# A two-layer transformer block beside a gated recurrence: the last product made token-major, the first root moved off GpSimd

## The chip, the cores and the metric

The kernel runs on one core of one Trainium2 chip. The metric is the device time of one execution in microseconds (us); the time before is the median of three runs. Profile names: PE is TensorE's matmuls, PEld its weight loads, DVE is VectorE, ACT is ScalarE, POOL is GpSimd, SP is SyncE, whose queue issues the DMAs. PSUM is the memory that TensorE writes and that DVE and ACT can read.

## The reference

The input `x` is 16 sequences of 512 tokens with 128 channels, in float32. What is computed, cut to the main lines:

```python
xn = layernorm(x)
# branch 1: gated recurrence
xc = causal_depthwise_conv(xn)                    # four taps
r, i = sigmoid(xc @ W_r.T + b_r), sigmoid(xc @ W_i.T + b_i)
a = sigmoid(log_a) ** (8 * r)
h[t] = a[t] * h[t-1] + sqrt(1 - a*a)[t] * (i * xc)[t]
s = rmsnorm(h @ W_out.T) * gamma
# branch 2: two layers of windowed attention (8 heads of 64, window 64) and a gated feed-forward block
for l in range(2):
    y = shift_token(z)                            # z starts as xn; half the channels one token later
    q, k, v = split(y @ wqkv[l])                  # q, k: l2norm, scale, rotary
    z = z + attention(q, k, v) @ wo[l]
    y = layernorm(shift_token(z)) * ln_g + ln_b
    a, g = split(y @ w1[l] + b1[l])               # 341 columns each
    z = z + (a * gelu(g)) @ w2[l] + b2[l]
return x + s * silu(z)
```

## The kernel before

The program is a list of 6240 tasks, each of them a few instructions of one engine. A task is a name and an item: a sequence `s` (0 to 15), a tile `(l, n)` of 128 tokens in layer `l`, a pair of tiles `(l, m)`, or a chunk `(c, s)` of the feed-forward block. The table `PLACES` gives each task its place in the list (the numbers are steps from one item to the next), written out in numbers; `OPENED` gives the PSUM bank of each tile (7 banks that all tiles share). The list is issued in this order, so each engine's queue runs its tasks in order, and an engine whose next task is not ready waits although later ones are.

What the change and the prediction touch:

- **Start of a sequence.** `ld` loads `xtok`. `fbn` and `fag` are DVE's statistics (4 and 4 small instructions, `fmv`). `fpw` (`deviation`, L589 to L593) makes 1/sqrt(var + eps) and -mean/deviation on POOL, in four instructions on 128x4, one of them a power. `fnm` (`normalised`, L600) scales on ACT in four pieces of 128x128 tokens by channels. `ftx` transposes on PE to channel-major, `xp` (L648) copies on ACT, `xs0` and `xs1` (L644) make the residual stream `xS` on POOL. `dr0` (L515, L516) computes `e` from `log_a` on ACT, `dr` (L520 to L531) the decay rate from it on DVE; both happen once.
- **Attention** of each tile: `Q`, `K`, `V` on PE (helper `matmul`, L636), squares on ACT, rotary products on DVE (L728, L731) and sums on POOL (`addq`, `addk`, L735), the normalisation of q and k on POOL (`nrm`, L772), flips on PE (`tr`, L793), scores, DVE's maxima (L840), ACT's exponentials (L847), POOL's shares (L861), `PT`, `PV`, and at last `wo` and `y` (L907), which adds to `xS`.
- **Feed-forward** of each sequence: `tx`, statistics, `pw`, `nm`, `nr`, `th`, `hT`; then for three chunks of hidden columns `g` and `a` (PE), `ge` (gelu, ACT), `hi` and for the last chunk `hj` (DVE, L952 and L957, tile `hid`), and `yy`, the second product (`narrow`, tile `1y` in layer 1). It is channel-major: `w2` is the stationary operand, the 512 tokens of `hid` stream through.
- **End of a sequence in layer 1.** `r0` and `r1` (`residual`, L970) add bias and stream to `1y`, half the channels each, into `lx`. `tf` (L631) transposes `lx` on PE into two banks, tokens on partitions. `silu` (L978, L980): ACT's tanh (`tn`) and DVE's product (`z`), once a bank, into `th`. `zs` and `zx` (`combine`, L987) multiply by `s` and add `x` on POOL. `xld` reloads `x`, one buffer for all sequences; `ot` (L990) stores.
- **Elsewhere:** `wide` (two masks and `gamma`) is loaded and cast by `cm` on POOL; `yo` (in `recurrent`, L636) is the recurrence's output product, token-major, with stationary `h` and 128 streaming columns.

Of the kernel before, what the change touches and what calls it, by code (L numbers as in the profile page):

```python
# [9 lines left out]
F32 = mybir.dt.float32  # L10
BF16 = mybir.dt.bfloat16
I32 = mybir.dt.int32
AF = mybir.ActivationFunctionType
# [27 lines left out]
    "dr0": "11",  # L41
    "dr": "15",
    "l1": "8",
    "t0": "31",
    "cm": "36",
    "l2": "30",
    "t1": "91",
    "wb0": "90",
    "bb0": "101",
    "ws0": "97",  # L50
    "wb1": "95",
    "bb1": "108",
    "ws1": "109",
    "ld": "0 1 11 5 24 159 161 50 1015 184 315 507 472 367 183 574",
    "fbn": "2 3 18 70 128 66 97 42 1027 214 283 539 437 370 178 610",
    "fag": "4 3 18 81 136 57 105 39 1270 53 198 625 541 219 129 655",
    "fpw": "6 3 18 121 103 53 112 30 1332 -8 197 730 530 124 133 713",
    "fnm": "10 4 20 158 162 49 1019 176 318 505 475 340 209 570 341 226",
    "ftx": "13 5 26 282 40 1023 190 303 450 526 371 204 554 351 206 502",
    "xp": "16 5 26 291 35 1020 194 297 454 525 379 195 554 351 205 502",  # L60
    "xs0": "19 5 55 303 40 987 182 328 452 500 378 364 438 434 203 446",
    "xs1": "22 11 215 391 -212 978 319 453 352 393 457 348 344 402 374 236",
    "c0": "26 2 61 258 41 1010 209 283 453 548 356 194 562 346 204 513",
    "cv": "20 38 101",
    "c1": "35 30 114 183 36 1008 207 284 450 552 360 188 561 352 202 511",
    "c3": "40 28 116 188 49 994 217 273 454 552 363 179 568 360 197 509",
    "gr": "46 34 241 154 119 857 247 272 413 555 350 220 525 379 199 535",
    "sr": "52 51 240 177 87 861 239 273 436 533 348 218 532 370 200 535",
    "gi": "55 20 182 123 188 877 199 297 423 564 352 210 555 350 206 497",
    "si": "59 23 184 121 197 871 196 305 439 551 340 210 579 328 207 493",  # L70
    "ea": "56 63 264 299 323 470 343 212 751 182 343 602 319 208 494 378",
    "in": "63 39 208 85 201 864 194 311 459 526 339 212 578 329 210 495",
    "a2": "70 63 307 265 367 416 355 246 742 144 348 714 197 297 426 399",
    "m": "84 166 195 295 346 507 269 348 670 138 396 745 83 526 211 452",
    "rt": "275 18 201 462 552 186 412 264 719 8 680 436 345 231 473 466",
    "u": "295 17 198 476 532 184 458 221 720 5 697 418 360 226 463 465",
    "sc": "306 26 248 422 521 185 500 183 723 94 607 411 362 243 466 449",
    "yo": "311 46 280 388 506 197 517 153 723 149 595 413 321 240 475 495",
    "s2": "320 48 284 383 503 195 520 160 714 151 603 404 321 240 474 501",
    "ms": "324 50 284 382 506 190 522 159 717 153 597 407 321 239 477 503",  # L80
    "mp": "331 55 284 375 523 178 514 163 721 146 603 418 310 236 475 521",
    "ss": "337 55 312 349 523 178 516 161 722 151 596 437 290 236 473 523",
    "c2": "365 41 1004 215 273 456 553 357 185 568 352 198 511",
    "Q": "29 10 66 13 23 9 73 16 41 178 76 67 102 65 86 64 146 50 91 64 169 58 141 32 167 90 117 59 102 108 116 69 "
    "98 67 105 58 178 57 112 50 180 86 90 66 88 51 132 49 135 145 115 86 120 64 110 18 125 122 114 44 90 132 102 33 "
    "-5071 40 75 62 121 52 85 75 130 62 92 62 186 61 110 118 131 52 98 77 172 60 91 48 135 53 99 33 187 48 136 129 "
    "136 59 74 78 165 6 105 59 231 42 106 68 166 43 106 48 181 53 90 66 137 67 116 45 216 -4 48 3 88 7 49 33",
    "sqq": "42 7 72 14 26 15 80 16 24 184 60 76 111 57 98 59 134 57 94 56 166 69 130 43 167 85 111 71 127 78 113 73 "
    "91 72 111 51 171 62 115 58 188 65 96 70 88 51 131 43 137 143 126 71 135 50 110 24 124 119 123 38 97 119 101 48 "
    "-5081 47 72 78 101 59 95 57 141 64 76 72 176 71 106 119 131 46 109 60 184 59 87 64 119 58 96 26 196 56 126 141 "  # L90
    "131 62 70 66 183 20 83 55 226 52 117 74 151 27 128 50 172 47 86 66 150 51 133 66 185 8 47 4 87 -4 51 45",
    "rq1": "48 -3 71 10 45 36 42 5 62 153 97 44 105 58 100 61 145 45 94 58 168 61 147 21 173 92 118 53 113 101 113 "
    "71 94 72 103 57 183 51 118 45 186 75 101 65 111 22 152 31 135 141 113 104 118 50 112 37 111 114 118 54 112 98 "
    "108 26 -5070 62 62 73 104 69 66 99 107 67 93 58 181 63 123 107 133 62 91 76 165 62 99 45 127 58 97 52 168 48 133 "
    "138 138 52 80 104 131 28 90 71 211 48 116 79 149 39 103 60 175 105 26 86 124 67 118 58 193 2 62 -10 92 6 47 57",
    "rq2": "38 22 53 10 51 35 22 28 54 150 97 48 101 69 82 66 144 51 95 61 165 67 133 42 160 90 114 72 94 105 128 59 "
    "97 67 109 57 172 56 117 60 177 76 93 91 86 23 138 45 143 141 112 94 114 63 106 43 104 119 120 55 100 129 78 36 "
    "-5070 46 87 41 120 62 75 75 144 65 76 71 178 63 126 106 123 81 76 74 168 66 85 61 133 69 84 27 183 54 130 130 "
    "136 64 89 68 164 -6 107 61 226 53 96 76 161 52 108 34 180 119 25 89 127 62 109 68 194 3 54 -4 85 6 47 42",
    "addq": "54 12 62 10 70 17 49 102 26 94 91 55 86 67 97 111 100 35 111 118 110 80 101 71 120 94 125 83 145 32 160 "  # L100
    "57 107 41 101 99 157 35 125 120 147 34 105 82 119 19 113 67 193 48 167 90 94 50 104 38 193 20 138 89 61 165 55 "
    "43 -5099 66 74 81 102 39 102 88 106 108 28 113 173 18 195 62 115 115 71 104 95 121 59 39 138 86 63 46 157 86 167 "
    "114 96 79 90 96 149 -28 96 157 135 49 121 127 79 63 157 105 53 110 46 100 121 42 130 110 144 -8 75 27 32 10 47 "
    "91",
    "K": "37 27 46 15 48 -18 78 13 40 175 86 74 96 55 115 53 129 51 94 59 168 62 137 69 138 85 114 70 111 89 133 53 "
    "98 69 111 52 195 41 111 54 187 75 90 82 68 65 118 58 130 145 151 61 107 65 107 24 123 118 131 31 94 125 101 39 "
    "-5076 46 90 47 126 42 88 74 132 69 80 80 168 65 130 98 127 54 98 74 182 50 102 40 132 65 87 44 178 58 133 128 "
    "143 45 79 97 147 24 83 66 225 45 113 59 167 38 117 45 182 53 83 68 136 64 116 60 202 -4 54 24 70 28 17 35",
    "sqk": "43 26 55 8 46 -3 85 10 30 183 84 59 104 59 116 39 134 49 94 57 179 75 121 66 157 87 96 70 115 80 133 67 "
    "81 70 116 47 205 34 109 81 172 63 89 86 85 56 125 39 144 141 140 61 108 85 87 40 117 119 124 31 90 124 119 28 "  # L110
    "-5066 44 77 59 127 41 81 70 136 74 79 69 167 75 132 89 139 60 80 75 202 43 98 57 112 78 73 45 170 58 148 118 143 "
    "50 81 94 142 32 83 64 222 40 120 75 154 29 131 30 197 39 90 69 131 77 127 54 176 2 52 21 69 47 3 52",
    "rk1": "57 20 43 31 43 -7 78 14 15 179 91 72 87 59 119 59 123 48 94 62 160 66 132 96 112 93 117 80 91 96 140 46 "
    "91 75 103 59 194 48 104 62 176 97 80 77 70 61 123 50 128 142 164 59 123 49 109 17 132 103 141 33 103 107 109 42 "
    "-5080 41 92 48 121 60 66 89 118 73 76 96 157 60 146 97 117 62 108 72 174 47 98 49 134 64 74 46 178 63 133 119 "
    "144 100 26 98 143 31 79 78 228 34 109 59 182 63 75 50 187 68 76 54 130 74 126 58 199 -8 70 7 67 45 17 38",
    "rk2": "50 31 55 17 32 6 80 -10 31 185 78 78 91 53 116 60 121 63 90 54 169 70 128 83 120 102 99 81 106 88 146 38 "
    "100 68 105 63 188 53 99 90 155 86 84 70 72 66 129 44 156 121 153 64 132 36 106 22 139 107 126 29 103 123 101 31 "
    "-5073 55 90 40 127 67 68 85 113 85 69 87 156 65 133 98 121 60 103 95 157 51 98 61 111 70 81 62 166 59 123 131 "
    "151 67 70 99 135 12 82 70 220 57 109 70 153 55 107 42 177 72 77 59 144 62 119 57 192 15 69 21 37 30 26 38",  # L120
    "addk": "61 24 58 15 55 5 63 116 -6 93 127 49 88 73 115 58 93 71 96 96 114 118 81 99 94 103 116 118 78 81 140 62 "
# [179 lines left out]
}  # L301

OPENED = {
    "wb0": "5",
    "wb1": "2",
    "ftx": "01232346010245104151450443430562",
    "c0": "3601015300330",
    "cv": "452",
    "gr": "4315262451000334",
    "gi": "3621315416303611",  # L310
    "yo": "3555154434312536",
# [816 lines left out]
```

## Time and profile before

| | |
|---|---|
| median of 3 runs | 1288.69 us (1287.65 to 1289.12) |
| the profiled execution's own time | 1286.86 us |
| its span, first to last instruction | 1285.1 us |
| granted TensorE clock, mean | 0.996 |
| busy: PE, ACT, DVE, POOL | 1244.4, 1164.9, 1112.3, 1081.9 us |

"Busy" is the time in which an engine works on at least one instruction. The profile writes each matmul of the program on float32 as two records, and the two column halves of a product run beside each other, so a mean duration of a record is longer than the distance between the starts of two. "Idle before, releaser" tells what ended an engine's wait. In the timeline each row is start, duration, engine, line, operation and tiles, with what ended the wait in brackets; instructions of one line that follow each other are merged (x2).

### The profile page before, as it was taken

What the parts mean: (1) busy time and instruction counts of PE and PEld (TensorE: products, weight loads), DVE (VectorE), ACT (ScalarE), POOL (GpSimd) and SP (SyncE); (2) the same over time, 40 slices, a digit from 0 to 9 for tenths busy, and PEclk for the clock granted to TensorE, in tenths of its full rate; (3) what the DMA queues carried; (4) which work ended last, traced back from release to release, by engine and by line L of the source; (5) the groups of instructions that cost most, each with busy time, mean ns of one, the idle gap of its engine ahead of it and who ended that gap; (6) DMA issues with size and microseconds to landing.
All of it is one profiled execution on the core that took longest, in us unless ns stands there. A gap on an engine that the chain in (4) does not pass through costs nothing.

```text
span 1285.1 us, 45136 instructions
## 1 busy us (share of the span) xinstructions
PE 1244.4 (97%) x17672; PEld 697.2 (54%) x17672; DVE 1112.3 (87%) x2866; ACT 1164.9 (91%) x3776; POOL 1081.9 (84%) x1057
## 2 busy tenths in 40 slices
PE   7899999999999999999999999999999999999997
PEld 2455565645645555555555555655465555665463
DVE  7999989888898989898899989969998888858964
ACT  5989999998999999998989999998999899998793
POOL 7999998986889889898788998868998798975792
PEclk9999999999999999999999999999999999999998
DMA  6211021111202101102121011211111021120111
GB/s 191 47 35 27 6 48 22 27 31 46 47 15 72 35 22 40 32 10 55 39 51 31 18 31 28 52 31 39 30 25 41 18 47 30 32 64 10 35 44 37
DMA packets 46771, 49.50 MB, mean 39 GB/s; under 512 B 4704, under 2 KB 31456, under 8 KB 46560
## 3 DMA queue, kind: packets, MB, share of 16 engines
q1 hardware_dynamic: 46560, 46.63, 15.0%
q8 instruction: 140, 2.29, 0.7%
q14 instruction: 71, 0.58, 0.1%
HBM read 13.05 MB, written 4.19 MB: 13 GB/s over the span
## 4 chain that ended last, share of the span: by engine, by line
PE 49%; DVE 18%; ACT 15%; POOL 12%; issue 4%; DMA 0%; POOLq 0%; DVEq 0%; ACTq 0%
ACT pr L847 7%; PE q L636 5%; PE o L882 5%; PE x L900 5%; PE v L636 4%; PE sA L834 4%; PE k L636 4%; POOL rot L735 3%; PE p L869 3%; POOL rot L772 3%; PE t L793 3%; DVE norms L740 3%; DVE max L840 2%; PE 0g L636 2%; POOL pr L861 2%
## 5 line engine op out<-in xcount | busy, mean ns | idle before, releaser
L735 POOL TENSOR_TENSOR rot<-rot,sw 128x512 f32<-128x512 f32 x256 | 326.9, 1289 | 27.7 <-DVE rot L728 11.0
L861 POOL TENSOR_TENSOR pr<-pr,sum 128x512 f32<-128x512 f32 x256 | 266.2, 1050 | 72.9 <-DVE sum L855 42.9
L772 POOL TENSOR_TENSOR rot<-rot,y 128x1024 f32<-128x1024 f32 x128 | 243.3, 1905 | 21.8 <-DVE y L767 20.5
L847 ACT ACTIVATE pr<-sB,max 128x128 f32<-128x128 f32 x512 | 188.8, 437 | 6.3 <-DVE max L840 4.5
L847 ACT ACTIVATE pr<-sA,max 128x128 f32<-128x128 f32 x512 | 188.4, 434 | 3.5 <-DVE max L840 2.6
L740 DVE TENSOR_REDUCE norms<-sq 128x16 f32<-128x1024 f32 x128 | 156.0, 1219 | 5.9 <-ACT sq L721 3.7
L873 ACT COPY pT<-p 128x512 f32<-128x512 f32 x256 | 143.4, 653 | 13.4 <-PE p L869 12.8
L882 PEld LDWEIGHTS o<-pT,vl 128*64 128x64 f32 x2048 | 111.7, 137 | 50.2 <-issue 26.6
L847 ACT ACTIVATION_READ_ACCUMULATOR pr<-sB,max 128x1 f32 x512 | 136.5, 276 | 0.0
L636 PE MATMUL q<-wqkv,xS 128*64 128x512 f32 x512 | 134.2, 608 | 1.3 <-DVE cols L916 0.4
L834 PE MATMUL sA<-kT,qT 64*64 64x128 f32 x2048 | 135.1, 269 | 0.0
L847 ACT ACTIVATION_READ_ACCUMULATOR pr<-sA,max 128x1 f32 x512 | 134.3, 273 | 0.0
L834 PE MATMUL sB<-kT,qT 64*64 64x128 f32 x2048 | 133.5, 269 | 0.0
L636 PE MATMUL v<-wqkv,xS 128*64 128x512 f32 x512 | 132.1, 600 | 0.7 <-ACT pr L847 0.7
L636 PE MATMUL k<-wqkv,xS 128*64 128x512 f32 x512 | 131.6, 596 | 0.2 <-ACT pr L847 0.2
L882 PE MATMUL o<-pT,vl 128*64 128x64 f32 x2048 | 127.6, 223 | 0.6 <-ACT pT L873 0.2
L882 PE MATMUL o<-pT,vs 128*64 128x64 f32 x2048 | 126.3, 222 | 0.0
L834 PEld LDWEIGHTS sA<-kT,qT 64*64 64x64 f32 x2048 | 121.0, 133 | 8.2
L900 PE MATMUL x<-oT,wo 128*64 128x257 f32 x1024 | 123.0, 382 | 0.5 <-ACT oT L890 0.3
L834 PEld LDWEIGHTS sB<-kT,qT 64*64 64x64 f32 x2048 | 120.1, 133 | 0.0
L840 DVE TENSOR_REDUCE max<-sA 128x4 f32<-128x512 f32 x128 | 86.9, 681 | 23.3 <-PE sB L834 16.2
L882 PEld LDWEIGHTS o<-pT,vs 128*64 128x64 f32 x2048 | 104.6, 138 | 0.2 <-ACT pT L873 0.2
(169 smaller groups left out, 3207.4 us busy)
## 6 DMA issues: line engine op xcount, KB each, us to landing
vl<-vs SPq DMA_DIRECT2D x224, 128.0 KB, 2.3
xtok<-in_x SPq DMA_DIRECT2D x16, 256.0 KB, 3.0
x<-in_x SPq DMA_DIRECT2D x16, 256.0 KB, 3.4
out<-th SPq DMA_DIRECT2D x16, 256.0 KB, 2.9
wqkv<-in_wqkv SPq DMA_DIRECT2D x2, 768.0 KB, 6.8
w<-in_w SPq DMA_DIRECT2D x2, 384.0 KB, 6.4
rot<-in_rope SPq DMA_DIRECT2D x1, 512.0 KB, 5.7
wo<-in_wo SPq DMA_DIRECT2D x2, 256.0 KB, 5.2
```

What stands on the lines that cost most here:

```text
L636: nc.tensor.matmul(ps[col : col + 64], w[:, col : col + 64], v, start=start, stop=stop)
L735: nc.gpsimd.tensor_tensor(r, r, at["sw", *n, "qk"[i]], ALU.add)
L740: nc.vector.tensor_reduce(at["nx", *pair(n)][:, 0, 16 * j : 16 * j + 16], sq, AX.X, ALU.add)
L772: nc.gpsimd.tensor_tensor(flat, flat, bc(at["y", *pair(n)][:, 0, 16 * j : 16 * j + 16], DH), ALU.mult)
L793: nc.tensor.transpose(four(at["bank", f"t{w}", *n])[:, i, p, :], r[rows, i, 2 * p : 2 * p + 2, :], c["ident"][rows, rows])
L834: nc.tensor.matmul(out_(w, par)[:, p, :], q[r, p, half[w]], k[r, p, col : col + P], start=False, stop=p == 3)
L840: nc.vector.tensor_reduce(at["max", *n, h], sim, AX.X, ALU.max, negate=True)
L847: nc.scalar.activation(at["pr", *n][:, g, :], sim[:, p, :], AF.Exp, bias=at["max", *n, h][:, p : p + 1], accum_out=at["sum", *n][:, g : g ...
L861: nc.gpsimd.tensor_tensor(w, w, bc(at["sum", *n][:, g], P), ALU.mult)
L873: nc.scalar.copy(at["pT", *n][:, w], heads(ps))
L882: nc.tensor.matmul(o[64 * par : 64 * par + 64, p, 64 * w : 64 * w + 64], at[("vl", "vs")[w], *n][:, h * DH : (h + 1) * DH], pT[:, w, 4 * p ...
L900: nc.tensor.matmul(ps[64 * r : 64 * r + 64, 0 : 2 * P + 1], w, o[:, k, 1 - r : 2 * P + 2 - r], start=k == 0, stop=k == 3)
```

## The change

1. In layer 1, `narrow` makes the second product token-major: `hid` is now stationary in pieces of 64 tokens, and the 128 columns of `w2` stream. The sum in the bank `1y` has tokens on partitions.
2. The transposes `tf` no longer follow the residual: they turn the stream `xS` before the second product, and a new DVE task `xt` adds the bias (now along the free dimension, `b2_row`) and keeps the result in `lx`. `r0` adds `lx` to the product in its bank; `r1` of layer 1 is gone. `tn` and `z` then work on all 512 columns at once, from `1y`.
3. For sequence 0 alone, `fpw` becomes `fq` (a square root on ACT) and `fr` (a reciprocal and a product on DVE); of the four pieces of the normalisation two stay on ACT (`fnm`) and two go to DVE (`fnd`).
4. For the last sequence alone, `zs` and `zx` run on DVE.
5. `wide` has a fourth part of 128 columns, the bias of layer 1, which POOL copies to `b2_row`; a constant `eps` is set.
6. All of `PLACES` and `OPENED` is written anew, so the order of all tasks is another.

The diff's core (the tables and the entries of `do` are left out):

```diff
-        add(s, ("ld", [("xtok", s)]), ("fbn", [("fmv", s)]), "fag", "fpw", ("fnm", [("xnf", s)]))
+        add(s, ("ld", [("xtok", s)]), ("fbn", [("fmv", s)]), "fag")
+        add(s, *(["fq", ("fr", [("xnf", s)]), "fnd", "fnm"] if s == 0 else ["fpw", ("fnm", [("xnf", s)])]))
...
-                add(C, (p + "yy", [] if c else [("bank", p + "y", s)] + [("lx", s)] * l))
-            add(s, p + "r0", p + "r1")
+                add(C, (p + "yy", [] if c else [("bank", p + "y", s)]))
+            if l:
+                add(s, ("tf", two("tf", s)), ("xt", [("lx", s)]), p + "r0")
+            else:
+                add(s, p + "r0", p + "r1")
...
+    def first_deviation(s, part):
+        mv = at["fmv", s]
+        r, o = mv[:, :, 2], mv[:, :, 3]
+        if part == 0:
+            nc.scalar.activation(r, mv[:, :, 1], AF.Sqrt, bias=eps)
+        else:
+            nc.vector.reciprocal(r, r)
+            nc.vector.scalar_tensor_tensor(o, mv[:, :, 0], -1.0, r, ALU.mult, ALU.mult)
+
+    def first_half(s):
+        mv, xn = at["fmv", s], at["xnf", s]
+        for t in range(2, NT):
+            nc.vector.tensor_scalar(xn[:, t, :], at["xtok", s][:, t, :], mv[:, t, 0:1], mv[:, t, 2:3], ALU.subtract, ALU.mult)
...
-            for t in range(NT):
+            for t in range(NT if s else 2):
                 nc.scalar.activation(xn[:, t, :], src[0][:, t, :], AF.Identity, bias=mv[:, t, 3:4], scale=mv[:, t, 2:3])
...
+        if l == 0:
+            return matmul(ps, w, hid, first, last)
+        for t in range(NT):
+            matmul(tok(ps)[:, t, :], hid[:, t * P : (t + 1) * P], w, first and t == 0, last and t == NT - 1)
...
+    def turn_stream(s):
+        for t in range(NT):
+            for r, ps in enumerate(two("tf", s)):
+                rows = slice(64 * r, 64 * r + 64)
+                nc.tensor.transpose(half(ps)[:, t], at["xS", s][rows, t * P + r : t * P + r + P], c["ident"][rows, rows])
+
+    def keep_stream(s):
+        for r, ps in enumerate(two("tf", s)):
+            b2 = b2_row[:, 64 * r : 64 * r + 64].unsqueeze(1).broadcast_to([P, NT, 64])
+            nc.vector.tensor_tensor(at["lx", s][:, :, 64 * r : 64 * r + 64], half(ps), b2, ALU.add)
+
+    def last_sum(s):
+        v = tok(at["bank", "1y", s])
+        nc.vector.tensor_tensor(v, v, at["lx", s], ALU.add)
...
+        th, v = at["th", s], tok(at["bank", "1y", s])
+        if i == 0:
+            nc.scalar.activation(th, v, AF.Tanh, scale=0.5)
+        else:
+            nc.vector.scalar_tensor_tensor(th, th, 1.0, v, ALU.add, ALU.mult)
...
+        engine = nc.vector if s == B - 1 else nc.gpsimd
+        engine.tensor_tensor(th, th, at[("s", "x")[i], s], (ALU.mult, ALU.add)[i])
```

The queues at the two ends, as the new places give them (task and sequence):

```
start, ACT:  fq0 fnm0 dr0 xp0 fnm1 xp1          before: fnm0 dr0 fnm1 xp0 xp1 fnm2
start, DVE:  fbn0 fag0 fbn1 fr0 fag1 fnd0 dr fbn2 fag2   before: fbn0 fag0 fbn1 fag1 dr fbn2 fag2
start, PE:   ftx0 cv0 ftx1 V Q K                before: ftx0 ftx1 cv0 Q V K
end, ACT:    ge(0,15) tn14 ge(2,15) ge(1,15) tn15
end, DVE:    r0 14, xt15, z14, hi(0..2,15) hj r0 15, z15, zs15, zx15
end, PE:     yy(0,14) tf15 th15 yy(1..2,14) g(2,15) g(0,15) a(0,15) g(1,15) a(1..2,15) yy(0..2,15)
```

## The prediction

> **What bounds the kernel now.** I read the page's busy line first, then the busy time in windows of 50 us, then the two ends in the timeline, then the waits of PE.
>
> ```profile
> span 1285.1 us, 45136 instructions
> PE 1244.4 (97%) x17672; PEld 697.2 (54%) x17672; DVE 1112.3 (87%) x2866; ACT 1164.9 (91%) x3776; POOL 1081.9 (84%) x1057
> 150.00:200.00 50.00, 49.92 (x808) 30.16 (x802) 44.42 (x113) 48.61 (x177) 45.46 (x41) 1.00 0.17 37
> 750.00:800.00 50.00, 48.32 (x644) 26.75 (x644) 45.92 (x110) 48.46 (x155) 43.29 (x39) 1.00 0.11 23
> PE t L793 <- POOL rot L772: 6.2, 11, 1.6
> PE tf L631 <- DVE lx L970: 3.2, 2, 1.7
> ```
>
> The windows' columns are time, length, then busy us of PE, PEld, DVE, ACT, POOL, the clock, DMA. TensorE is the bound, with three engines close behind it. From 100 to 1250 us it is idle 14.8 us in all: 0.64 us in a mean window of 50 us, with a standard deviation of 0.52, from 0 to 1.82. Its 40.7 idle us lie mostly at the ends: 16.3 in the first 100 us and 9.5 after 1250. So either the ends get shorter, or TensorE's work or its idle time between them changes.
>
> The end, in the timeline (start, duration, engine, line):
>
> ```profile
> 1273.85 0.75 DVE L957 SCALAR_TENSOR_TENSOR hid<-1g,cols,gelu 21x512 f32<-21x512 f32 x1
> 1275.78 1.51 DVE L970 SCALAR_TENSOR_TENSOR lx<-1y,cols,xS 64x512 f32<-64x512 f32 x2 [1.18 <-PE 1y L636]
> 1277.44 0.46 PE L631 MATMUL tf<-squares,lx 64*128 64x64 f32 x8 [1.71 <-DVE lx L970]
> 1277.95 0.66 ACT L978 ACTIVATE th<-tf 128x256 f32<-128x256 f32 x2 [5.79 <-issue]
> 1278.37 0.75 DVE L980 SCALAR_TENSOR_TENSOR th<-th,tf 128x256 f32<-128x256 f32 x2 [1.08 <-ACT th L978]
> 1279.20 1.26 POOL L987 TENSOR_TENSOR th<-th,s 128x512 f32<-128x512 f32 x1 [4.98 <-DVE th L980]
> 1280.54 1.26 POOL L987 TENSOR_TENSOR th<-th,x 128x512 f32<-128x512 f32 x1
> 1281.83 0.37 SPq L990 DMA_DIRECT2D out<-th  x1
> ```
>
> Nothing overlaps here: residual, transposes, tanh, product, two POOL passes, store. From the last matmul of `1y` (1275.73) to the store's issue it is 6.10 us.
>
> The start:
>
> ```profile
> 4.83 0.23 POOL L589 TENSOR_SCALAR fmv<-fmv 128x4 f32<-128x4 f32 x1 [3.44 <-DVE fmv L583]
> 5.15 1.04 POOL L590 TENSOR_TENSOR fmv<-fmv,mhalf 128x4 f32<-128x4 f32 x1
> 6.84 1.65 ACT L600 ACTIVATE xnf<-xtok,fmv 128x128 f32<-128x128 f32 x4 [1.92 <-POOL fmv L593]
> 8.85 0.15 DVE L521 TENSOR_SCALAR z<-e 128x1 f32<-128x1 f32 x1 [3.02 <-ACT e L516]
> 10.59 1.44 ACT L648 COPY xp<-fx 128x256 f32<-128x256 f32 x4
> ```
>
> POOL's small operations hold the first normalisation. DVE's decay-rate chain waits for ACT's `e`. The copy `xp` of sequence 0 stands behind sequence 1's normalisation in ACT's queue.
>
> **The change part by part.** The profiled execution took 1286.86 us (span 1285.1), 1.83 below the median 1288.69 of the three runs. I sum differences on its trace and apply the sum to the median.
>
> *The end.* I keep the last matmul of `1y` at 1275.73 and count 0.05 for each hop between engines. The sum `r0` is one DVE operation with one PSUM operand, 128x512: 0.68 by L728, to 1276.46. The tanh is one ACT operation, 0.725 by L669, to 1277.24. The product is one DVE operation, 0.744 by L952, to 1278.03. The two passes now follow on DVE with no hop. L537 has both operands in SBUF, 1.215 for 1024 columns; I take 0.68 each, nearer the 512-column rows than half of it. They end at 1279.4, and the store goes out 2.4 us earlier. Ahead of it, DVE's `hid` operations of sequence 15 started when `z` of 14 was through (1271.52). By the new queue, `r0` of 14 (0.68 from 1267.5), ACT's tanh (behind one gelu, 1269.9 to 1270.6) and `z` (0.75) bring this to about 1271.35: 0.2 earlier. Together -2.6. Bounds: -1.3 (every DVE pass 0.2 longer, `hid` 0.5 later) to -3.1 (hops hidden). What is late next is the load of `x` for sequence 15. One buffer serves all, so it stays behind the store of 14 (issued 1274.72) and lands about 3.1 us later, at 1277.8; the pass that needs it starts at 1278.7. If that 0.9 is used up, the pass waits.
>
> *The second product.* Before, 12 records of 512 columns a sequence; after, 48 of 128 columns, with four times the weight loads.
>
> ```profile
> 314.24 1.04 PE L636 MATMUL yo<-squares,h 128*64 128x128 f32 x16
> L636 PE MATMUL 1y<-hid,w 128*64 128x512 f32 x128 | 33.3, 602 | 0.0
> L636 PE MATMUL 1y<-hid,w 85*64 85x512 f32 x64 | 16.7, 600 | 0.0
> ```
>
> `yo` has exactly the new shape. Its 16 records take 1.04, of which the last one's own 0.27 is fill: 0.77 for 15 starts, 51 ns each. Records of 512 columns start every 215 ns (four in 0.86). So 48 x 0.053 equals 12 x 0.215, about 2.55 us, and the lower bound is 0. Upper bound: `yo`'s busy sum is 17.9 us for 16 groups, 1.12 a group; three groups in each of 16 sequences are 53.7, against 33.3 + 16.7 = 50.0, so +3.7. I take +0.5, near the start-to-start row, since PE's queue is full around these groups. The Trainium skill, page "TensorE: Matmul & The Clock Gate", section "Back-to-back issue gap", speaks against this change: in a stream of weight loads and matmuls it puts 128 columns at about 81 ns and 512 at about 131. By that the sum would be 16 x (48 x 81 - 12 x 131) ns, 37 us more, an estimate from that page. The 51 and 215 ns of this trace contradict both figures.
>
> *The stream's transposes.* As many as before (8 a sequence, 0.46), but they read `xS` before the second product is through, so PE no longer waits for DVE's `lx`. Outside the end that wait is 1.5 us, once. I count -1.0 of it, since PE's next task may be late itself. The new DVE copy `xt` waits for those transposes; queued behind it are maxima and reciprocals that ACT and POOL need. It costs nothing as long as PE ran the transposes well before, as in the queue of sequence 14; if not, 0.4 each time.
>
> *DVE, ACT and POOL in between.* DVE a sequence: 2 x 0.75 + 2 x 0.414 = 2.33 before; 2 x 0.415 (L603) + 0.68 + 0.744 = 2.25 after. ACT: 2 x 0.411 becomes one of about 0.70. Over 16 sequences that is 1.3 and 1.9 us less, on engines that TensorE covers: 0. If TensorE were not the cover, they would be a gain.
>
> *The start.* Root first:
>
> ```profile
> L687 ACT ACT_TABLE_LOAD x14 | 18.0, 1283 | 0.2
> L847 ACT ACT_TABLE_LOAD x21 | 26.9, 1283 | 4.3 <-DVE max L840 4.0
> ```
>
> Every Sqrt group (L687) needs a table load, and L847's loads stand behind a wait for DVE. So the root waits for the statistics (4.75), then 1.28 for the table and 0.2 (L516) for itself: 6.3. Reciprocal and product (0.16 and 0.19, L522 and L763) bring 6.7. The halves run side by side, ACT's to 7.6 (before 8.49). Then ACT's `e` needs the other table back: 9.3, against 8.82. `xp` of sequence 0 now stands ahead of sequence 1's normalisation: 9.35, against 10.59. So PE's convolution starts 1.2 earlier. But DVE's decay-rate chain, sequence 2's statistics behind it and POOL's third root (14.10) come 0.5 later. POOL also has one more small copy (`b2_row`, 0.29 to 0.53 by L540 and L544) ahead of its first rotary sum. So the start lies between -1.2 (TensorE decides) and +0.9 (POOL decides). TensorE idles 16 us in the first 100 us, so neither must arrive whole: I take 0. The larger `wide` load (+64 KB) delays only the loads behind it, of which sequence 2's input was first used at 12.8: 0.
>
> *The order.* All places are new. PE's tasks keep their sequence nearly (half move by one place or less), and the trace can't price this. Were the windows' idle times drawn anew, the sum of 23 would have a standard deviation of 0.52 x 4.8 = 2.5 us: 0, give or take 2.5.
>
> Sum: -2.6 + 0.5 - 1.0 + 0 = -3.1. That is a median of 1285.6.
>
> **The rivals.** *A better order too.* If the new places also bring the six worst windows (8.1 us idle) to the mean (3.9), 4.2 go besides: 1281.4. For it: the worst window, 1200 to 1250 (1.82), holds the last sequences' second products, which the change touches. Against: nothing in the change aims at the other five.
>
> *A worse order (the other side).* PE's flips of q and k wait for POOL's normalisation, in 11 waits of up to 1.6 us now; POOL's queue is as full as TensorE's in places. Four more such waits are 6.4 us: 1288.7 - 3.1 + 6.4 = 1292.0. It makes the kernel measurably slower from 5.7 us of added PE idle time between 100 and 1250 us. Against: the distance from a normalisation to its flip in the list of tasks is the same in both orders (median 14 and 15 places).
>
> *The product at full price.* +3.7 instead of +0.5: 1288.8, no change. For it: weight loads fourfold. Against: `yo`.
>
> **How the numbers follow.** Measurements of this kernel tell about 0.2% (2.6 us) from no change, so faster means below 1286.1, slower above 1291.3. Forecast 0.60, with its 2.5 either way: 0.36 faster, 0.22 same, 0.02 slower; its own range is 1282.4 to 1288.8. Better order 0.17, faster. Worse order 0.14, slower. Full price 0.09: 0.06 same, 0.03 slower. So 0.53, 0.28, 0.19. The range, 1281.0 to 1291.5, leaves out the lower part of the better order and the upper half of the worse one.
>
> **What would show it.** Right: the store about 3.7 us after the last `1y` matmul instead of 6.1; groups of 16 `1y` records of 1.0 to 1.1 us; a table load ahead of the first root and one ahead of `e`, `xp` near 9.4; PE idle of 12 to 18 us between 100 and 1250. Wrong: `1y` records starting over 60 ns apart, the last pass waiting for `x`, or PE idle over 20 us there.

## The result, and the profile after

The changed kernel took 1280.81 us (median of 4 runs, 1279.31 to 1282.47), the kernel before 1288.17 (1287.63 to 1289.12) on the same chip: ratio 0.9945 [0.9934, 0.9957]. The forecast was 1285.6, from a time before of 1288.69; taken from there, the ratio gives 1281.6, at the lower edge of the stated range (1281.0 to 1291.5). That is the time of the rival "a better order too" (1281.4). The profiled execution took 1280.66 us, 6.2 less than the profiled one of before, so 6.2 us are to be found between the two traces.

The page of the changed kernel, busy line:

```profile
span 1278.9 us, 46290 instructions
PE 1241.5 (97%) x18248; PEld 725.6 (57%) x18248; DVE 1114.4 (87%) x2872; ACT 1164.5 (91%) x3759; POOL 1076.2 (84%) x1053
```

PE's busy time fell by 2.9 us although it streams as many columns as before; its idle time fell by 3.3 (40.7 to 37.4). The end in the timeline, from the last product on:

```profile
1268.79 3.20 PE L661 MATMUL 1y<-w,hid 128*64 128x128 f32 x47
1272.04 0.70 DVE L1014 TENSOR_TENSOR 1y<-1y,lx 128x512 f32<-128x512 f32 x1 [1.20 <-PE 1y L661]
1272.82 0.60 ACT L1021 ACTIVATE th<-1y 128x512 f32<-128x512 f32 x1 [4.44 <-DVE 1y L1014]
1273.45 0.69 DVE L1023 SCALAR_TENSOR_TENSOR th<-th,1y 128x512 f32<-128x512 f32 x1 [0.71 <-ACT th L1021]
...
1275.62 0.37 SPq L1034 DMA_DIRECT2D out<-th  x1
```

The last `1y` matmul ends at 1271.99, the store goes out 3.63 us later (6.10 before). The start, ACT's timeline: a table load ahead of the root (6.31), another ahead of `e`, and the first `xp` at 9.45:

```profile
5.01 1.28 ACT L610 ACT_TABLE_LOAD   x1 [5.01 <-DVE fmv L593]
6.31 0.30 ACT L610 ACTIVATE fmv<-fmv,eps 128x4 f32<-128x4 f32 x1
...
8.05 1.28 ACT L525 ACT_TABLE_LOAD   x1
...
9.45 0.76 ACT L673 COPY xp<-fx 128x256 f32<-128x256 f32 x2
```

PE's waits, and one window of 50 us (columns as in the prediction):

```profile
PE t L818 <- POOL rot L797: 6.4, 8, 2.3
PE 0y L661 <- DVE hid L977: 2.7, 1, 2.7
```

```profile
1050.00:1100.00 50.00, 46.69 (x658) 26.95 (x655) 46.91 (x104) 42.39 (x132) 37.74 (x36) 0.97 0.15 36
```

PE was idle 13.0 us between 100 and 1250 (14.8 before), but 3.3 of them in this one window, in a wait that the kernel before doesn't have.

**Where the 6.2 us went.** Idle time alone doesn't tell it, so I give every matmul its column time: 215 ns for 512 columns and so in proportion, and half of that for the records on 64 rows and 64 columns, which run two beside each other. Lost is what the start of a matmul lies behind the column time that PE has issued until then. These weights add up to 1127 us in both kernels. The table's add up to 1137.6, 1% more; with all weights scaled to that sum its entries come out within 0.6 us, and the differences between kernels within 0.5. Lost us in stretches of column time, from one trace of each of five kernels (the last three are experiments below). The last row is the whole time from there to the span's end, with 12.6 us of column time in it:

| stretch of column time | before | after | old list, both of PE's edits | new list, old product | new list, memset moved |
|---|---|---|---|---|---|
| 0 to 200 | 42.2 | 43.3 | 42.6 | 41.8 | 42.8 |
| 200 to 950 | 77.4 | 67.4 | 78.0 | 70.2 | 66.7 |
| 950 to 975 | 1.2 | 6.3 | 1.3 | 8.2 | 1.6 |
| 975 to 1125 | 15.7 | 15.6 | 15.9 | 15.4 | 15.4 |
| from there to the span's end | 23.6 | 21.3 | 22.4 | 21.2 | 21.3 |

After against before: +1.1, -10.0, +5.1, -0.1, -2.3, together -6.2. The two edited ends are small. A long middle lost 10 us less, and one place, near 1065 us in the trace, gave 5 back. Experiments 5 to 8 show that both belong mainly to the list.

### The profile page after: what moved, and what is told of

Same layout as the page of the kernel before. It is cut to its first block, busy times and chain, and to the rows that moved or that the text cites. A ratio compares the mean times of both kernels' runs of the same rounds, so it can differ in the third digit from the quotient of the medians.

```text
span 1278.9 us, 46290 instructions
## 1 busy us (share of the span) xinstructions
PE 1241.5 (97%) x18248; PEld 725.6 (57%) x18248; DVE 1114.4 (87%) x2872; ACT 1164.5 (91%) x3759; POOL 1076.2 (84%) x1053
## 4 chain that ended last, share of the span: by engine, by line
PE 59%; DVE 17%; ACT 15%; POOL 5%; issue 3%; DMA 1%; SPq 0%; ACTq 0%; DVEq 0%; POOLq 0%
ACT pr L872 6%; PE q L661 6%; PE o L907 6%; PE v L661 6%; PE k L661 5%; PE x L925 5%; PE sA L859 5%; PE t L818 4%; PE p L894 4%; PE 1y L661 2%; PE 0g L661 2%; DVE max L865 2%; DVE rot L753 2%; DVE sw L756 2%; PE 1g L661 2%
## 5 line engine op out<-in xcount | busy, mean ns | idle before, releaser
L872 ACT ACTIVATION_READ_ACCUMULATOR pr<-sB,max 128x1 f32 x512 | 139.2, 281 | 0.0
L818 PEld LDWEIGHTS t<-squares,rot 64*128 64x128 f32 x2048 | 74.9, 140 | 45.1 <-POOL rot L797 18.4
```

The lines of the kernel that those rows point to most:

```text
L818: nc.tensor.transpose(four(at["bank", f"t{w}", *n])[:, i, p, :], r[rows, i, 2 * p : 2 * p + 2, :], c["ident"][rows, rows])
L872: nc.scalar.activation(at["pr", *n][:, g, :], sim[:, p, :], AF.Exp, bias=at["max", *n, h][:, p : p + 1], accum_out=at["sum", *n][:, g : g ...
```

## Experiments

"Old list" is the order of the kernel before, "new list" that of the changed one. Each ratio is to the kernel before on the same chip.

**1 and 2. Edits without the list, the list without the edits.** All edits in the old list; and the new list with all edits undone. Because the edits change which tasks there are, I had to place some by hand (`tf` and `xt` where two banks were free, `tn` and `z` soon after `r0`, some two dozen other tiles to other banks in the first). In the second, six sequences' residual reads the buffer of `xS` after the list has handed it to the sequence five later; the amount of work is the same.

```diff
 old_list_all:   PLACES, OPENED of before, edits 1 to 5 of the change
 new_list_none:  PLACES, OPENED of the changed kernel
-                edits 1 to 4 of the change (5, the wider load and its copy, stays)
```

> All edits of the change (product, transposes, root, last passes) in the list of the kernel before: every old task keeps its place there, tf and xt are put in where two banks are free, 28 tiles change their bank. Theory A (the rewritten list brings what the forecast lacked, about 4 us between 100 and 1250 us): this kernel gets only the end's -2.6 and about -0.5 from the transposes, so 1284 to 1287 us. Theory B (the token-major product itself frees the middle): 1280 to 1282.5 us, as the changed kernel. The hand-made places can cost up to 2 us under either.

> The list of the changed kernel with every edit undone: channel-major product, residual into lx, transposes tf behind it, root of sequence 0 on POOL, last passes on POOL; r1 and tf are put in behind r0. Theory A: the list alone gives -4, so 1283 to 1285.5 us. Theory B: the list alone gives nothing, 1287 to 1290 us.

Measured: 1308.23 us, ratio 1.0166 [1.0153, 1.0179], and 1308.22, 1.0160 [1.0147, 1.0173]. Both fail both theories. In the 200 to 950 stretch they lost 95.0 and 89.1 us (77.4 before). Both kernels took some 21 us more than the kernel before, ten times the 2 us that I had allowed for placing tasks by hand. Experiments 5 to 7, which leave every task in its place, have no such loss, so I put it down to the places and banks chosen by hand; no run takes these apart. So the two say nothing of the change's parts. They do show one link: the new list starts six of the sequences in a buffer that is free only because `tf` reads the stream early.

**3. The last passes back on POOL.**

```diff
-        engine = nc.vector if s == B - 1 else nc.gpsimd
+        engine = nc.gpsimd
```

> The changed kernel with the last sequence's two passes back on POOL. Under both theories only the end moves: 2 x (1.27 - 0.69) and a hop or two, so 1.2 to 1.4 us slower than the changed kernel, about 1282.1 us, with the store 1.3 us later behind z.

Measured: 1280.71 us, 0.9946 [0.9933, 0.9960]. From the end of `z` to the store it took 2.71 us instead of 1.48, the 1.23 that the rows promised; the total doesn't resolve it. The two traces differ in the clock at the start: TensorE ran at 0.83 to 0.84 in two windows of 10 us before 60 us in the changed kernel, and at 1.00 in all of them here.

**4. The first root back on POOL, all of the normalisation on ACT.**

```diff
-        add(s, *(["fq", ("fr", [("xnf", s)]), "fnd", "fnm"] if s == 0 else ["fpw", ("fnm", [("xnf", s)])]))
+        add(s, "fpw", ("fnm", [("xnf", s)]))
-            for t in range(NT if s else 2):
+            for t in range(NT):
```

> The changed kernel with sequence 0's root and its whole normalisation back on POOL and ACT (fpw, four pieces on ACT). If TensorE's start decides, 0.5 to 1.2 us slower than the changed kernel (about 1281.7); if POOL's chain decides, up to 0.9 us faster (about 1280.2). One table load fewer on ACT at the start. The forecast took the start at 0.

Measured: 1280.75 us, 0.9944 [0.9932, 0.9955]: no difference from the changed kernel. The first `xp` came at 9.18, earlier than with the root on ACT (9.45). Edit 3 is worth nothing that these runs resolve.

**5 to 7. The product's form and the transposes, each task in its own place.** Only what a task issues is changed.

```diff
 old_product_rows, in the kernel before:
-        matmul(at["bank", f"{l}y", C[1]], w, hid, C[0] == 0, C[0] == KCH - 1)
+        if l == 0: return matmul(ps, w, hid, first, last)
+        for t in range(NT):
+            matmul(tok(ps)[:, t, :], hid[:, t * P : (t + 1) * P], w, first and t == 0, last and t == NT - 1)
 old_product_rows_stream, besides:
-        "tf": lambda s: token_major(two("tf", s), at["lx", s]),
+        "tf": turn_stream,      # reads xS, in tf's old place
 new_product_channels, in the changed kernel:
+        matmul(at["bank", f"{l}y", C[1]], w, hid, C[0] == 0, C[0] == KCH - 1)
-        (the loop over t)
```

> The kernel before with one edit: in layer 1 the second product is issued in the new form (stationary pieces of hid, 128 streaming columns), in the old places; residual and transposes read it as before, so the sum mixes tokens and channels. It prices the term second product by itself. The prediction's term is +0.5 us (bounds 0 and +3.7): ratio to the kernel before 1.0004 (1.000 to 1.003). Theory product (the new form is itself what makes the middle of the kernel denser): 3 us or more less, ratio 0.998 or below. Theory list (the gain in the middle comes from the new places, which suit the new tasks): the same 1.000 to 1.003 as the prediction.

> The same, and besides the transposes tf read the stream xS instead of the residual's result, still in their old places behind it, so that TensorE no longer waits for DVE's lx; the second product of layer 1 thus has no part in the output. Old list, both of TensorE's edits. Prediction: +0.5 - 1.0 = -0.5 us (-2.0 to +2.7), ratio 0.9996. Theory list: the same, the remaining 5 to 10 us of the middle come only with the new places. Theory product and transposes: most of the gain in the middle is here already, 5 us or more less, ratio 0.996 or below.

> The changed kernel with one edit undone: the second product of layer 1 is issued in the old form (stationary w2, 512 streaming columns), in the new places; the sum adds a token-major stream to a channel-major product. Prediction: 0.5 us below the changed kernel (1280.8 - 0.5 = 1280.3; bounds 1277.1 and 1280.8), ratio to the kernel before 0.994. Theory list: the same. Theory product: 3 us or more above the changed kernel, 1284 or more, ratio 0.9968 or above.

Measured: 1287.64 us, ratio 1.0007 [0.9998, 1.0016]; 1286.53, 0.9996 [0.9987, 1.0004]; 1282.72, 0.9965 [0.9951, 0.9979]. In the old list the two edits together are worth half a microsecond, and the middle stays as it was (78.0 lost, 77.4 before). With the old product the new list still loses only 70.2 there. That kernel keeps the transposes of the stream, which in the old list, in `tf`'s old place, moved nothing in the middle. So the list, with what the early transposes allow it, makes most of the gain of the middle, 7 of 10 us. The remaining 2.8 us lie almost wholly at one place, near 815 us, where `o` waits for a DMA (old product in the new list, then the changed kernel):

```profile
815.02 0.34 PE L907 MATMUL o<-pT,vl 128*64 128x64 f32 x4 [2.43 <-DMA vl<-vs]
815.15 0.34 PE L907 MATMUL o<-pT,vl 128*64 128x64 f32 x4 [1.14 <-DMA vl<-vs]
```

From 815 to 820 us the mean clock was 0.66 in the first and 1.00 in the second. Whether the old product causes that wait is not shown: the medians are 2 us apart by the ratios, but the intervals overlap. The other place where the old product loses more is the stall at 1065.

Of the 10 us, 1.8 lie where the kernel before has the long scan of experiment 10 (column time 550 to 575), which takes 1.28 us in the new list; moving that scan alone in the old list takes as much away there. The rest is spread over the middle.

The size of experiment 6 is the forecast's, but the transposes did not earn it where the forecast had put it. The wait of 1.46 us for `lx` at 655.77 (in the kernel before) is still there when `tf` reads the stream, now with another releaser of DVE's queue:

```profile
655.77 0.46 PE L631 MATMUL tf<-squares,lx 64*128 64x64 f32 x8 [1.46 <-DVE lx L970]
656.56 0.46 PE L981 MATMUL tf<-squares,xS 64*128 64x64 f32 x8 [1.51 <-DVE sum L855]
```

What went is the other wait for `lx`, 1.7 us at the end (the table's last row: 22.4 against 23.6). As for the product, its rows in the changed kernel (the groups of 16 that stand alone took 1.04 to 1.09 us):

```profile
L661 PE MATMUL 1y<-w,hid 128*64 128x128 f32 x512 | 32.9, 275 | 0.0
L661 PE MATMUL 1y<-w,hid 85*64 85x128 f32 x256 | 16.9, 274 | 0.0
```

One thing that fell with the list is the waits of PE's weight loads. Kernel before, then the changed one, in the waits of all engines (total us, times, longest):

```profile
PEld t L793 <- POOL rot L772: 28.1, 34, 2.5
PEld p L869 <- POOL pr L861: 17.5, 26, 1.2
```

```profile
PEld t L818 <- POOL rot L797: 18.4, 24, 3.1
PEld p L894 <- POOL pr L886: 12.2, 19, 1.0
```

The sum of the two is 45.6 before, 44.8 with the edits in the old list, 35.1 in the new list with the old product, 30.6 in the changed kernel; the lost time of the middle is 77.4, 78.0, 70.2 and 67.4. But the two do not go together everywhere: experiments 1 and 2 have 42.2 and 38.4 us of these waits and lost 95.0 and 89.1. So they are at most a part of the cause, and what else made the middle lose less stays open.

**8. The stall at 1065 us.** In the changed kernel's timeline:

```profile
1059.92 6.21 DVE L1051 TENSOR_TENSOR_SCAN h<-thr,thi 128x512 f32<-128x512 f32 x1
1060.70 1.90 POOL L797 TENSOR_TENSOR rot<-rot,y 128x1024 f32<-128x1024 f32 x1
1062.56 1.27 POOL L760 TENSOR_TENSOR rot<-rot,sw 128x512 f32<-128x512 f32 x1
1063.79 1.26 POOL L1031 TENSOR_TENSOR th<-th,x 128x512 f32<-128x512 f32 x1
1066.06 0.72 DVE L977 SCALAR_TENSOR_TENSOR hid<-0a,cols,gelu 128x512 f32<-128x512 f32 x1
1066.83 1.80 PE L661 MATMUL 0y<-hid,w 128*64 128x512 f32 x4 [2.73 <-DVE hid L977]
```

The recurrence's scan takes 1.21 us where POOL leaves room; this is that of sequence 14. Here POOL worked without a gap until 1065.05, and the scan ended at 1066.13, 1.08 us later: I read that it stood until then. `hid` stood behind it in DVE's queue, PE waited 2.73 us for `hid`, and its next four records took 1.80 instead of 1.03, because the clock fell (mean 0.71 from 1065 to 1070). The Trainium skill, page "SBUF — State Buffer", section "Who interferes with whom", says that a VectorE instruction with two SBUF inputs, as this scan has, excludes a GpSimd instruction that reads SBUF and the other way round, and that an instruction that only writes is no hindrance. So I moved a memset of POOL's into that stretch:

```diff
 new list:
-  ... vz(1,48) ... vd(1,48) vd(1,49) ... addk(0,60) ... sc 14 kz(1,25) sim(1,49) nrm(0,59)
+  ... addk(0,60) ... sc 14 vz(1,48) kz(1,25) vd(1,48) vd(1,49) sim(1,49) nrm(0,59)
```

> The changed kernel with GpSimd's memset of a v tile (vz of tile pair 1,48, 0.52 us, and the two DMAs behind it) moved eight places down, to just behind the scan of sequence 14 in the list, so that GpSimd does not run two-operand work without a gap from 1056 to 1065 us. Theory scan (VectorE's scan stands until GpSimd has a gap or does a memset: it took 6.21 us instead of 1.21, TensorE waited 2.73 us for the hid behind it and then ran at half clock for 3.4 us): the scan falls to 1.3 to 2.0 us, the wait of 0y for hid goes, and the time falls by 2.7 to 4.4 us, to 1276.4 to 1278.1, ratio 0.991 to 0.992. Rival (the scan is long for a reason of its own, or another wait takes its place): the scan stays above 4 us or the time stays within 1 us of 1280.8, ratio 0.994.

Measured: 1274.48 us (1274.05 to 1274.92), ratio 0.9902 [0.9888, 0.9915], some 5.5 us below the changed kernel by the ratios (0.9902 against 0.9945, each uncertain by 1.5 to 1.7 us), more than the 2.7 to 4.4 expected. Its timeline:

```profile
1058.66 0.52 POOL L835 MEMSET vl<- 64x512 f32 x1
1058.72 1.44 DVE L1051 TENSOR_TENSOR_SCAN h<-thr,thi 128x512 f32<-128x512 f32 x1
1059.13 1.23 POOL L806 COPY kT<-kT 128x256 f32<-128x256 f32 x1
```

The scan got in, POOL's copy waited for it in its turn (1.23 us, else 0.39), the wait of `0y` is gone, and the stretch from 950 to 975 lost 1.6 instead of 6.3. So the scan's standing and its price, about 5 us, are shown; why the scan came in here is not (see experiment 9).

**9 and 10. The same in the old list.** The kernel before has such a scan too, at 649.14 (sequence 9), and DVE's `lx`, for which `tf` waited 1.46 us at 655.77, stands in the queue behind it:

```profile
649.14 4.47 DVE L1006 TENSOR_TENSOR_SCAN h<-thr,thi 128x512 f32<-128x512 f32 x1
654.20 1.51 DVE L970 SCALAR_TENSOR_TENSOR lx<-1y,cols,xS 64x512 f32<-64x512 f32 x2
```

First I moved a memset there, then, since that did nothing, the scan itself.

```diff
 old_memset_moved:
-  vz(0,36) vd(0,36) ... addk(0,38) rq2(1,30) sc 9 addq(0,38)
+  ... addk(0,38) vz(0,36) rq2(1,30) sc 9 addq(0,38) vd(0,36)
 old_scan_moved:
-  rq2(1,30) sc 9 addq(0,38) rk2(1,30) nrm(1,29) 1r1 5 1r0 5 rB rA rk1(1,30) fpw 12
+  rq2(1,30) addq(0,38) rk2(1,30) nrm(1,29) 1r1 5 1r0 5 rB rA rk1(1,30) sc 9 fpw 12
```

> The kernel before with one memset moved in its list: vz of tile pair (0,36) and the DMA behind it go some 25 places down, to between the two rotary sums that ran beside the scan of sequence 9 (649 us; it took 4.47 us, and TensorE then waited 1.46 us for DVE's lx at 655.8). Theory scan (the scan stands until GpSimd has a gap or does a memset, in any order of tasks): the scan falls below 1.8 us, the wait of tf for lx goes, and the time falls by 1.5 to 3.0 us, ratio 0.9977 to 0.9988. Rival (TensorE's tasks there wait for something else as well, or the scan's length is its own): the ratio stays within 0.9993 to 1.0007.

> The kernel before with the scan of sequence 9 moved 18 places down its list, behind the residual's two instructions and three small ones, to where GpSimd has the small instructions of a root next. Theory scan (the scan stands behind GpSimd's two-operand work that has no gap, and what waits is VectorE's queue behind it): the scan starts near 652.2 us and takes 1.2 to 1.8 us instead of 4.47, the 1.46 us wait of tf for lx goes, and the time falls by 1.5 to 3.0 us, ratio 0.9977 to 0.9988. Rival (TensorE's tasks there wait for something else as well): the scan is short and the ratio stays within 0.9993 to 1.0007.

Measured: 1287.26 us, 1.0002 [0.9993, 1.0011], and 1285.66, 0.9989 [0.9980, 0.9998]. In the first the scan began while the memset ran, and still took 4.64 us, because the sum behind the memset went ahead of it: the theory was too simple there, and so the run doesn't test what the scan costs. Experiment 8 agrees with the page's sentence on instructions that only write; this run doesn't show it.

```profile
649.02 4.64 DVE L1007 TENSOR_TENSOR_SCAN h<-thr,thi 128x512 f32<-128x512 f32 x1
```

In the second (timeline, then PE's waits):

```profile
653.97 1.46 POOL L593 TENSOR_TENSOR fmv<-fmv 128x4 f32<-128x4 f32 x1
654.22 1.21 DVE L1007 TENSOR_TENSOR_SCAN h<-thr,thi 128x512 f32<-128x512 f32 x1
```

```profile
PE tf L632 <- DVE lx L971: 1.7, 1, 1.7
```

The scan takes 1.21, this time POOL's small instruction stands behind it (1.46 instead of 0.20), and of the two waits for `lx` only the one at the end is left. The gain, 1.4 us, is a little under the expected 1.5 to 3.0.

**11. The changed kernel with both repairs:** the memset moved, and the root back on POOL, but the normalisation shared as in the change.

```diff
-["fq", ("fr", [("xnf", s)]), "fnd", "fnm"] if s == 0
+[("fpw", [("xnf", s)]), "fnd", "fnm"] if s == 0
```

> The changed kernel with the memset moved as in new_memset_moved, and with the first root back on GpSimd (four small instructions, ready near 7.0 us), but the normalisation of sequence 0 still shared by ScalarE and VectorE. Theory start (the root on ScalarE costs two table loads and delays e and the decay-rate chain; the split is what helps): xp of sequence 0 near 8.5 us instead of 9.45, DVE's chain near 8.4 instead of 9.6, and 1.2 to 2.0 us less than new_memset_moved (1274.5 on its chip, ratio 0.9902), so a ratio of 0.9887 to 0.9893. Rival (the start is decided by something else): the ratio of new_memset_moved, 0.990, or above.

Measured: 1273.39 us (1272.69 to 1273.78), ratio 0.9894 [0.9881, 0.9908], the lowest of all. The first `xp` starts at 8.65 and DVE's chain at 8.33, as expected; but the ratio lies between the two theories' (0.9887 to 0.9893, and 0.990 or above), and the interval overlaps that of experiment 8, so a gain from the second repair is not shown.

## Why the prediction was right or wrong

- **The end, -2.6:** right. -2.3 from column time 1125 on, the store 3.63 us after the last product against the 3.7 foretold. The load of `x` landed at 1274.32, before the pass that needs it (1274.90).
- **The second product, +0.5 (0 to +3.7):** right in the old list, +0.9 (1.0007, interval -0.3 to +2.1 us). The groups of 16 records took 1.04 to 1.09, and the busy sum is 32.9 + 16.9 = 49.8 against 50.0. `yo` was the right row to price it by, and the rival of the full price is out.
- **The transposes, -1.0:** the size came (1.0007 to 0.9996, 1.4 us by the ratios and 1.1 by the medians, each ratio uncertain by 1.1), but by luck. The term was the wait outside the end, and with `tf` on the stream that wait stayed (1.51 us, experiment 6); what went in that trace lay at the end, which the prediction counts in another term. The wait outside the end came from the scan in front of `lx`: moving the scan removed it and gained 1.4 us.
- **The start, 0 (-1.2 to +0.9):** right. +1.1 up to column time 200 in this trace, with two dips of the clock before 60 us; -0.4 in the trace of experiment 7, with the same start and no dip.
- **The order, 0 give or take 2.5:** this is the step that failed. The new places were worth -7 to -10 us in the middle and +5 at the scan. The 2.5 came from the spread of PE's idle time over windows, and idle time shows only part of what is lost: it fell by 1.8 us between 100 and 1250 where the lost time, by the table, fell by about 5. A part of the rest may be in the weight loads' waits for POOL, 45.6 us in the kernel before, which the prediction did not read; which part stays open. The second miss is of kind: windows drawn anew don't allow for one place with a stall of 5 us of its own.
- **The rivals:** "a better order too" came within 0.6 us of the time, partly by luck. Its reason, that the six worst windows become mean ones, came in part: their idle time fell from 8.1 to 5.0 us, not to 3.9. But the window of the stall rose by 2.6 in turn, and most of the gain lies in lost time that is not idle time. "A worse order" named POOL's normalisation; the wait that came was 2.73 us for DVE, behind the scan, and the waits for POOL became fewer.

## What to carry to other kernels

Where a list of tasks is rewritten with an edit, compare the lists by the lost time of the bounding engine (start times against issued work), not by its idle time alone. Look in both traces for single instructions that last several times their usual duration: here one scan held 5 us, and moving one memset (with two DMAs) down the list, past the scan, gave three quarters as much again as the whole change had gained. To test an edit apart from its list, keep every task in its place and change only what it issues.

## What the runs showed of the hardware that I had not expected

- VectorE's scan of two SBUF operands took 1.21 us, or up to 6.21 beside GpSimd's work, ending 1.08 us after the last GpSimd instruction that went ahead of it. Three instructions in a row went ahead at 649 us (before), five at 1060 us (after). It is not kept out by every such row: in the kernel before, at 771 us, it came in after one instruction although GpSimd's next followed without a gap, and that one stood instead (the two of the last line took 3.42 us together, 2.49 in a row elsewhere):

```profile
770.67 1.04 POOL L861 TENSOR_TENSOR pr<-pr,sum 128x512 f32<-128x512 f32 x1 [1.16 <-DVE sum L855]
771.09 1.70 DVE L1006 TENSOR_TENSOR_SCAN h<-thr,thi 128x512 f32<-128x512 f32 x1
771.67 3.42 POOL L735 TENSOR_TENSOR rot<-rot,sw 128x512 f32<-128x512 f32 x2
```

- A memset on GpSimd let the scan in once (experiment 8) and once not (experiment 9, 4.64 us). What decides which engine comes first, here and at 771 us, stays open.
- After a wait of 2.73 us TensorE ran slower than full speed: four records of 512 columns took 1.80 us instead of 1.03. After one of 2.43 us the mean clock was 0.66 for 5 us, after one of 1.14 us it was 1.00. So the two longer waits cost more than their own length.
